# A fused S5 block and attention layer: a constant moved from the projection's weights to the inverted softmax divisors, two rows made in two periods, and the opening's last period moved by one

## The chip, the cores and the metric

The kernel runs on one core of a Trainium2 chip. The core has five engines with an instruction queue each: TensorE for matrix products (PE in the profile; PEld are its weight loads), VectorE (DVE), ScalarE (ACT), GpSimd (POOL) and SyncE (SP), which here issues all DMA transfers. The metric is device time in microseconds (us) of one execution. The kernel before takes 3392.98 us, the median of 3 runs that span 3391.85 to 3394.76 us.

## The reference

Input x is (2, 2048, 512), two sequences of 2048 rows, with a condition vector of 512 for each. The first layer is a state-space block with a feed-forward part. The second layer, whose last stages the change touches, is attention with a layer norm whose scale and shift depend on the condition:

```python
h = _sln(hidden, w, ...)                      # layer norm, * gamma(w) + beta(w)
q, k, v = split of h @ Wqkv.T + bqkv          # 16 heads of 32
energy = einsum('bhqd,bhkd->bhqk', q, k)
att = softmax(energy, axis=-1) / D ** 0.5     # D = 512: after the softmax
out = einsum('bhqk,bhkd->bhqd', att, v)
out = out @ Wp.T + bp
h1 = out + hidden
h2 = _sln(h1, w, ...)                         # the same gamma and beta again
return h2 + h1
```

The factor 1/sqrt(D) comes after the softmax. It is a plain constant on the result of attention, and can be multiplied in anywhere between the softmax and the sum with `hidden`.

## The kernel before

**The opening half.** The S5 block, its feed-forward part and the projections to q, k and v go over 8 chunks of 512 rows, 4 for each sequence. It ends a little after 1340 us. What is left then of the projections (4 value tiles of the chunk before the last, then for the last chunk 4 transposed feature tiles, 8 tiles of keys and queries and 4 value tiles: 20 pieces in the list `left`) is done in the first periods of the attention, beside it.

**Attention.** A block is one sequence, one pair of heads and one chunk of 512 queries; there are 2 * 8 * 4 = 64 blocks. Each block needs 16 tiles of scores (128 keys by two heads by 512 queries). Since fp32 scores need a maximum before the exponential, the scores are made ahead:

- `keep` (line 863) makes a score tile on TensorE (`raw_scores`, line 853), copies it to memory on ScalarE (line 867) and takes the running maximum on VectorE (line 872). Eleven of 16 tiles are kept so.
- `compare` (line 874) does the maximum only, for the other five (line 876). These five are made a second time later, in `make` (line 906), which takes the maximum off while VectorE reads the scores (line 910).
- `turn_run` (line 878) transposes the running maximum on TensorE (line 884) and reduces it on VectorE (line 885), for each head of the pair. `spread` (line 889) transposes the 8 rows of maxima (`pt_neg`, line 892), copies them on ScalarE (line 894), writes them to DRAM (`flat`, line 896) and reads them back to all partitions (`shift`, line 898).
- `take_off` (line 902) adds `shift` to a kept tile on GpSimd (line 904), `exponentials` (line 913) is ScalarE's exp (line 915), and `weighted` (line 918) is the product with the values on TensorE (line 925), with a column of ones, so that the softmax divisor comes out of the same product. The last product of a block is copied out (line 934), and its sums and rows go to DRAM (lines 938, 941).

**Periods.** The order of the work on all engines is written out by hand: a loop over periods j (line 1311), 8 periods to a block (`NP = 8`), with the scores made 14 periods ahead of the products (`AHEAD = 14`). Each engine takes its instructions in this order. Within a period: what `after` put there (`run_due(j)`, line 1329), `make`, `compare`, the first exponential, the kept tiles, then pieces of `left`, the second exponential, what `closing` put there (`run_due(j + 0.5)`, line 1356), `take_off` for the next period and `weighted` for the last one. The loop starts at j = -22; block n has its products from j = 8n on. At `j == OPEN`, with `OPEN = -4`, the memory of the first half is given back (line 1314), new pools are opened, and two value tiles get their ones (line 1323). The pieces of `left` are spread evenly over the periods up to `OPEN` (line 1346). For block 0, `turn_run` is due in j = -5 and -4, and `spread` in j = -3.

**The end of each sequence.** When all heads of a chunk of queries are done, `fetch_sums` (line 953) reads the 16 x 512 divisors back as a 128 x 64 tile; `invert` (line 961), two periods later, takes their reciprocal on VectorE (line 963) and writes it to DRAM (line 964). `fetch`, `divide` and `project` (lines 975 to 1006) read attention's rows and the inverse divisors, multiply them on GpSimd, and project with `wp` on TensorE. `last_rows` (line 946) makes two tiles of 128 equal rows from the layer norm's scale and shift: `along_rows` (line 166) is 4 matmuls that spread columns along rows (line 170) into a PSUM tile and one ScalarE copy (line 174). In this stage that PSUM tile has the tag `pt`, of one buffer, which `turn_run`, `spread` and `project` use too. `last_rows` comes in period 272 for the first sequence (ahead of the period's scores) and in period 483 for the second, where a `turn_run` and an `invert` are due as well. The last chunk of all has its own `end_*` functions: its last pair of heads is divided straight from PSUM in `end_last` (line 1151; lines 1162 and 1164).

**The weights.** `wp`, the 512 x 512 projection laid out as 128 x 2048, is loaded in period 22 (line 1326), and in period 32 GpSimd multiplies all of it by 1/sqrt(D) (line 1328).

Of the kernel before, what the change touches and what calls it, by code (L numbers as in the profile page):

```python
# [8 lines left out]
F32 = mybir.dt.float32  # L9
# [5 lines left out]
ALU = mybir.AluOpType  # L15
# [4 lines left out]
P = 128  # L20
# [19 lines left out]
def tile_s5_block_then_sln_attention(  # L40
# [21 lines left out]
    nc = tc.nc  # L62
    NB, L, D = x.shape
    KC = D // P
# [7 lines left out]
    NQ = L // CH  # L72
# [25 lines left out]
    s_scale = const.tile([P, KC, NB], F32, name="s_scale")  # L98
    s_shift = const.tile([P, KC, NB], F32, name="s_shift")
# [66 lines left out]
    def along_rows(dst, cols, psum, tag):  # L166

        pt = psum.tile([P, CH], F32, name="pt_ar", tag=tag)
        for k in range(KC):
            nc.tensor.matmul(  # L170
                pt[:, k * P : (k + 1) * P], cols[k].to_broadcast([P, P]), ident,
                start=True, stop=True,
            )
        nc.scalar.copy(dst, pt)
# [501 lines left out]
    pt = ps1.tile([P, KC, CH], F32, name="pt_s", tag="po", bufs=1)  # L676
# [266 lines left out]

    held, ending = {}, {}

    def last_rows(b):
        g_row = rows.tile([P, D], F32, name="g_row", bufs=1)
        along_rows(g_row, [s_scale[:, k, b : b + 1] for k in range(KC)], ps, "pt")
        t_row = rows.tile([P, D], F32, name="t_row", bufs=1)
        along_rows(t_row, [s_shift[:, k, b : b + 1] for k in range(KC)], ps, "pt")  # L950
        ending[b] = g_row, t_row

    def fetch_sums(b, c, heads=slice(0, NH), width=64):

# [6 lines left out]
    def invert(b, c, heads=slice(0, NH), width=64):  # L961
        sm = held.pop((b, c, "sm"))
        nc.vector.reciprocal(sm, sm)
        nc.sync.dma_start(invd[b][heads, c * CH : (c + 1) * CH].rearrange("h (s i) -> h s i", i=width), sm)

    def store(b, qt, rows):
# [184 lines left out]
    def end_last(o):  # L1151
        raw, inv = (spare(n)[:, 0, :] for n in ("raw4", "inv4"))
        on = ends["o"][1][:, 1, :]
        turned = ps.tile([P, 2, 2 * P], F32, name="turned", tag="pt")
        parts = [slice(2 * i * P, 2 * (i + 1) * P) for i in range(2)]
        for at in parts:
            nc.scalar.copy(raw[:, at], o[:, at])
        end_begin(1)
        for i, at in enumerate(parts):
            nc.tensor.matmul(turned[:, i, :], ends["turn"], raw[:, at], start=True, stop=True)  # L1160
        for i, at in enumerate(parts):
            nc.vector.reciprocal(inv[:, at], turned[:, i, :])
            for r in (slice(0, HD), slice(3 * HD, P)):
                nc.vector.tensor_tensor(on[r, at], o[r, at], inv[r, at], ALU.mult)
        end_project(1, list(range(NG - 1)))
        mv = small.tile([P, TT, 2], F32, name="mv4")
        g_row, t_row = ending[LB]
        for i in range(2):
            for t in (2 * i, 2 * i + 1):
                nc.tensor.matmul(  # L1170
                    ends["py", i][:, t % 2, :], on[:, t * P : (t + 1) * P], ends["w"], start=False, stop=True
                )
            for t in (2 * i, 2 * i + 1):
                st = small.tile([P, 6], F32, name="st3")
                nc.vector.bn_stats(st, ends["py", i][:, t % 2, :])
                nc.vector.bn_aggr(mv[:, t, :], st)
        v = small.tile([P, TT], F32, name="v4")
        scale = small.tile([P, TT], F32, name="scale4")
        nc.vector.tensor_scalar(v, mv[:, :, 1], EPS, None, ALU.add)
        nc.vector.tensor_scalar(  # L1180
            scale.bitcast(I32), v.bitcast(I32), -0.5, float(0x5F3759DF), ALU.mult, ALU.add
        )

        nc.gpsimd.tensor_scalar(v, v, -0.5, None, ALU.mult)
        for _ in range(3):
            c = small.tile([P, TT], F32, name="c4")
            nc.gpsimd.tensor_tensor(c, scale, scale, ALU.mult)
            nc.gpsimd.tensor_tensor(c, c, v, ALU.mult)
            nc.gpsimd.tensor_scalar(c, c, 1.5, None, ALU.add)
            nc.gpsimd.tensor_tensor(scale, scale, c, ALU.mult)  # L1190
        ws, hts = [spare("w01"), spare("w23")], [spare("ht01"), spare("ht23")]
        for t in range(TT):
            h = ends["py", t // 2][:, t % 2, :]
            w, ht = ws[t // 2][:, t % 2, :], hts[t // 2][:, t % 2, :]
            nc.vector.scalar_tensor_tensor(w, h, mv[:, t, 0:1], g_row, ALU.subtract, ALU.mult)
            nc.vector.tensor_tensor(ht, h, t_row, ALU.add)
        for t in range(TT):
            qt = LC * TT + t
            w, ht = ws[t // 2][:, t % 2, :], hts[t // 2][:, t % 2, :]
            nc.vector.scalar_tensor_tensor(ht, w, scale[:, t : t + 1], ht, ALU.mult, ALU.add)  # L1200
            nc.sync.dma_start(out[LB, qt * P : (qt + 1) * P, :], ht)
# [6 lines left out]
    NP = 8  # L1208
# [20 lines left out]
    def after(j, what, *args):  # L1229

        due.setdefault(j, []).append((what, args))

    def closing(j, what, *args):

        due.setdefault(j + 0.5, []).append((what, args))

    N = len(blocks)
    FIRST = -AHEAD - 8
    OPEN = -4
    for i, n in enumerate(opens):  # L1240
        free = NP * (max(m for m in range(N) if pair_of[m] == i - 2) + 1) if i > 1 else FIRST
        after(max(free if i > 1 else FIRST, NP * n - 26), load_k, i)
        after(max(OPEN + 2, NP * n - 9), load_v, i)
    for n in range(N):
        after(max(FIRST + 1 + n, NP * n - 21), load_q, n)
        after(NP * n - AHEAD + NP + 1, turn_run, n, 0)
# [2 lines left out]
    for b in range(NB):  # L1249
        for c in range(NQ):  # L1250
            j = NP * (blocks.index((b, NPAIR - 1, c)) + 1) + 1
            if (b, c) == (LB, LC):
                most, rest = slice(0, NH - 4), slice(NH - 4, NH - 2)
                j = NP * (N - 1)
                after(j - 5, fetch_sums, b, c, most)
                after(j - 3, invert, b, c, most)
                for g in range(NG - 1):
                    after(j - 2 + g, end_sums, g)
                after(j + 1, end_weights)
                after(j + 1, end_sums_more)  # L1260
                after(j + 2, end_x)
                after(j + 1, fetch_sums, b, c, rest, 32)
                after(j + 4, invert, b, c, rest, 32)
                after(j + 5, end_divisors, NG - 1, 2, 1)
                for g in range(NG - 1):
                    after(j + 3 + g, end_divide, g)
                for e in (1, 2):
                    after(j + 8, end_divide, NG - 1, slice(HD * e, HD * e + HD))
                after(j + 6, end_begin, 0)
                for g in range(NG - 1):  # L1270
                    after(j + 6 + g // 2, end_project, 0, [g])
                continue
            after(j, fetch_sums, b, c)
            after(j + 2, invert, b, c)
            if c == 0:
                after(j + 2, last_rows, b) if b == LB else after(NP * (NPAIR * NQ * (b + 1) + 2), last_rows, b)
            for t in range(TT):
                qt = c * TT + t
                if b == LB:
                    k = j + 3 + 2 * t  # L1280
                    after(k, fetch, b, qt)
                    after(k + 2, divide, b, qt)
                    after(k + 3, project, b, qt)
                    after(k + 3, residual, b, qt)
                    after(k + 3, statistics, b, qt)
                    after(k + 4, deviation, b, qt)
                    after(k + 5, last_norm, b, qt)
                    after(k + 6, last_close, b, qt)
                else:

                    k = NP * (NPAIR * NQ * (b + 1) + 2 + 3 * qt // 2)
                    after(k, fetch, b, qt)
                    after(k + 3, divide, b, qt)
                    for g in range(NG):
                        closing(k + 5 + g // 2, project, b, qt, (g,))
                    closing(k + 7, residual, b, qt)
                    closing(k + 8, statistics, b, qt)
                    closing(k + 9, gain, b, qt)
                    after(k + 11, turns, b, qt)
                    closing(k + 12, scaled, b, qt)  # L1300
                    after(k + 14, close, b, qt)
# [9 lines left out]
    for j in range(FIRST, NP * N + 2):  # L1311
# [12 lines left out]
            wp = fixed.tile([P, KC, D], F32, name="wp")  # L1324
        if j == 2 * NP + 6:
            nc.sync.dma_start(wp, w_pT.rearrange("(k p) f -> p k f", p=P))
        if j == 4 * NP:
            nc.gpsimd.tensor_scalar(wp, wp, ISQ, None, ALU.mult)
        run_due(j)
        n, i = block_at(j + AHEAD)  # L1330
        todo = list(keeps[i]) if n is not None else []
# [90 lines left out]
```

## Time and profile before

| | |
|---|---|
| median of 3 runs | 3392.98 us (3391.85 to 3394.76) |
| the profiled execution | 3393.83 us, of which its span is 3392.1 us |
| mean granted clock of TensorE | 0.992 |
| busy share of the span | PE 97%, DVE 65%, POOL 62%, ACT 58% |
| attention: first product with the values | at 1422.9 us of the span |
| GpSimd's `take_off`, line 904 | 704 instructions, mean 2390 ns |
| scores, line 856 / products, line 925 | 2688 matmuls, mean 427 ns / 4096 matmuls, mean 611 and 597 ns |
| multiplication of `wp`, line 1328 | 1 instruction, 5369 ns, at 1531.7 us |
| rows of `last_rows`, ScalarE's copies | at 2382.9 and 2384.7, 3201.4 and 3203.3 us |
| reciprocals of `invert`, line 963 | 9 instructions, median 543 ns |
| division in `end_last`, line 1164 | 4 instructions, 412 to 430 ns, from 3372.4 us |

How to read the profile: a page has the busy time of each engine over the span, slices, the chain that ended last, and groups of instructions with a mean duration and the idle time before them. A timeline lists instructions in order of time. Its columns are the start and the time in us, the engine, the line of the kernel, the operation, what is written and read, the shapes and the count; a bracket at the end gives how long the engine sat idle before it, and what it waited for. Matmuls in a timeline are pipelined, so a group's time reaches somewhat into the next one's.

### The profile page before, as it was taken

Reading aid. Unit: us, or ns where it says so; the run is one execution under the profiler, and the core shown is the slowest. Engines: PE = TensorE matmul, PEld = TensorE weight load, DVE = VectorE, ACT = ScalarE, POOL = GpSimd, SP = SyncE. Lnnn points to the kernel's source line nnn. Section 1 sums busy time; section 2 is a strip of 40 time slices with the busy share of each in tenths; the row PEclk is TensorE's granted clock in tenths of the full one; section 3 lists DMA queues with packets and bytes.
Section 4 is the critical chain, followed back from the end, with each engine's and each line's share of the span. In section 5 each row is a group of like instructions: output and inputs, shape, how many; then the busy total and the mean of one; then the engine's idle time right before and its main releaser. Section 6 shows DMA issues by size and latency. Waiting matters only on the chain.

```text
span 3392.1 us, 33637 instructions
## 1 busy us (share of the span) xinstructions
PE 3294.7 (97%) x11076; PEld 1417.8 (42%) x11076; DVE 2218.2 (65%) x2792; ACT 1951.0 (58%) x2210; POOL 2117.6 (62%) x1164
## 2 busy tenths in 40 slices
PE   7999999999999999999999999999999999999987
PEld 4444444444444444443444444444444434443432
DVE  5352525252525212688888888888888888888884
ACT  2111111111111111598999999999888888888852
POOL 2341313131313111399999999999899999989885
PEclk9999999999999999999999999999999999999998
DMA  8022221222222212332313231323233243243233
GB/s 298 25 50 71 53 75 49 78 57 71 62 62 56 59 47 75 113 85 61 74 49 74 67 74 49 75 68 75 70 92 90 67 95 88 65 90 83 63 102 97
DMA packets 249781, 259.07 MB, mean 76 GB/s; under 512 B 94920, under 2 KB 167112, under 8 KB 245510
## 3 DMA queue, kind: packets, MB, share of 16 engines
q1 hardware_dynamic: 249606, 256.92, 28.5%
q8 instruction: 88, 1.44, 0.2%
q14 instruction: 87, 0.71, 0.1%
HBM read 166.77 MB, written 67.76 MB: 69 GB/s over the span
## 4 chain that ended last, share of the span: by engine, by line
PE 62%; DVE 15%; ACT 15%; issue 3%; POOL 2%; DMA 2%; SPq 0%; DVEq 0%; ACTq 0%; POOLq 0%
PE ph L538 13%; PE po L551 13%; PE o L925 10%; DVE run L872 8%; PE s L856 8%; ACT x L867 7%; PE pk L587 6%; ACT x L915 4%; ACT pT L915 4%; PE pv L599 3%; DVE pT L910 3%; PE py L1005 2%; POOL x L904 2%; DVE run L876 2%; PE pu L474 2%
## 5 line engine op out<-in xcount | busy, mean ns | idle before, releaser
L904 POOL TENSOR_TENSOR x<-x,shift 128x1024 f32<-128x1024 f32 x704 | 1654.9, 2390 | 134.1 <-DMA shift<-flat 117.1
L856 PE MATMUL s<-qs,ks 128*128 128x512 f32 x2688 | 824.8, 427 | 39.4 <-DVE run L872 26.6
L867 ACT COPY x<-s 128x1024 f32<-128x1024 f32 x704 | 692.2, 1011 | 142.9 <-PE s L856 137.1
L872 DVE TENSOR_TENSOR run<-s,run 128x1024 f32<-128x1024 f32 x576 | 705.2, 1224 | 81.7 <-ACT x L867 37.1
L915 ACT ACTIVATE x<-x 128x1024 f32<-128x1024 f32 x704 | 738.8, 1059 | 15.7 <-POOL x L904 15.4
L925 PE MATMUL o<-x,v 128*64 128x512 f32 x2816 | 717.2, 611 | 1.2 <-ACT x L915 1.2
L856 PEld LDWEIGHTS s<-qs,ks 128*128 128x128 f32 x2688 | 444.1, 189 | 454.7 <-DVE run L872 158.0
L538 PE MATMUL ph<-fT,w_sb 128*128 128x512 f32 x1024 | 459.4, 592 | 0.9 <-ACT fT L682 0.9
L551 PE MATMUL po<-w_sb,hid 128*128 128x512 f32 x1024 | 460.0, 592 | 0.0
L542 ACT ACTIVATE hid<-ph,vec 128x512 f32<-128x512 f32 x128 | 87.8, 686 | 614.7 <-PE ph L538 614.7
L910 DVE TENSOR_TENSOR pT<-s,shift 128x1024 f32<-128x1024 f32 x320 | 388.9, 1215 | 52.6 <-PE s L856 52.2
L876 DVE TENSOR_TENSOR run<-s,run 128x1024 f32<-128x1024 f32 x320 | 389.3, 1216 | 12.1 <-PE s L856 11.6
L915 ACT ACTIVATE pT<-pT 128x1024 f32<-128x1024 f32 x320 | 339.5, 1061 | 89.9 <-DVE pT L910 89.6
L561 POOL TENSOR_TENSOR x<-x,gated 128x512 f32<-128x512 f32 x32 | 39.6, 1269 | 506.5 <-DVE gated L560 506.5
L925 PE MATMUL o<-pT,v 128*64 128x512 f32 x1280 | 332.0, 597 | 15.2 <-ACT pT L915 15.2
L164 DVE SCALAR_TENSOR_TENSOR lo<-pk,vec,hi 128x512 fp32r<-128x512 f32 x64 | 47.8, 746 | 423.0 <-ACT hi L163 423.0
L551 PEld LDWEIGHTS po<-w_sb,hid 128*128 128x128 f32 x1024 | 194.4, 190 | 243.9 <-issue 243.7
L538 PEld LDWEIGHTS ph<-fT,w_sb 128*128 128x128 f32 x1024 | 194.1, 190 | 243.3 <-issue 239.2
L925 PEld LDWEIGHTS o<-x,v 128*64 128x64 f32 x2816 | 157.0, 135 | 311.7 <-issue 239.3
L163 ACT ACTIVATE hi<-pk,vec 128x512 fp32r<-128x512 f32 x64 | 44.0, 687 | 373.4 <-PE pk L587 373.4
L524 POOL TENSOR_TENSOR x<-x,gated 128x512 f32<-128x512 f32 x28 | 35.4, 1264 | 255.3 <-DVE gated L523 255.3
L925 PEld LDWEIGHTS o<-pT,v 128*64 128x64 f32 x1280 | 91.6, 138 | 200.2 <-issue 142.2
(280 smaller groups left out, 2449.3 us busy)
## 6 DMA issues: line engine op xcount, KB each, us to landing
ks<-kd SPq DMA_DIRECT2D x128, 256.0 KB
qs<-qd SPq DMA_DIRECT2D x512, 64.0 KB
shift<-flat SPq DMA_DIRECT2D x64, 512.0 KB
moved<-fT SPq DMA_DIRECT2D x224, 64.0 KB
x<-in_x SPq DMA_DIRECT2D x8, 1024.0 KB
w_sb<-in_w SPq DMA_DIRECT2D x8, 1024.0 KB
kd<-hi SPq DMA_DIRECT2D x32, 256.0 KB
kd<-lo SPq DMA_DIRECT2D x32, 256.0 KB
```

The costliest lines, as they stand in the source:

```text
L538: nc.tensor.matmul(ph, w1_sb[:, k, f * P : (f + 1) * P], fts[b, c][:, k, :], start=k == 0, stop=k == KC - 1)
L551: nc.tensor.matmul(pos[b, c][:, t, :], hid[:, t * P : (t + 1) * P], w2_sb[:, f, :], start=f == 0, stop=f == FC - 1,)
L587: nc.tensor.matmul(pk, w[:, k, g * P : (g + 1) * P], hT[:, k, :], start=k == 0, stop=k == KC - 1)
L599: nc.tensor.matmul(pv, fts[b, c][:, k, t * P : (t + 1) * P], wv[:, k, :], start=k == 0, stop=k == KC - 1)
L856: nc.tensor.matmul(s[:, e, :], kst[pair_of[n], e][:, kt * P : (kt + 1) * P], qst[n][:, e, :], start=True, stop=True,)
L867: nc.scalar.copy(x, s)
L872: nc.vector.tensor_tensor(runs[n], s, kept[n, 0] if kt == 1 else runs[n], ALU.max)
L876: nc.vector.tensor_tensor(runs[n], raw_scores(n, kt), runs[n], ALU.max)
L904: nc.gpsimd.tensor_tensor(x, x, shifts[n], ALU.add)
L910: nc.vector.tensor_tensor(x, s, shifts[n], ALU.add)
L915: nc.scalar.activation(x, x, AF.Exp)
L925: nc.tensor.matmul(outs[n][64 * e : 64 * e + 64, :], v[:, kt, e : e + 2, :], x[:, e, :], start=first, stop=final,)
```

## The change

Four edits. The multiplication of `wp` by `ISQ` = 1/sqrt(D) is gone; `invert` multiplies the reciprocals by `ISQ`, and `end_last` multiplies by it in its own division. `last_rows` becomes `last_row`, called once for each row: the first in the closing part of period k, the second in the closing part of period k + 1, where k is 272 for the first sequence, as before, and 481 for the second, two periods ahead of before. `OPEN` goes from -4 to -3, so that the pieces of `left` have one period more, and the pools of the attention are opened one period later; the first loads of values stay in period -2 (`OPEN + 1` in place of `OPEN + 2`).

```diff
-    def last_rows(b):
-        g_row = rows.tile([P, D], F32, name="g_row", bufs=1)
-        along_rows(g_row, [s_scale[:, k, b : b + 1] for k in range(KC)], ps, "pt")
-        t_row = rows.tile([P, D], F32, name="t_row", bufs=1)
-        along_rows(t_row, [s_shift[:, k, b : b + 1] for k in range(KC)], ps, "pt")
-        ending[b] = g_row, t_row
+    def last_row(b, name, columns):
+        row = rows.tile([P, D], F32, name=name, bufs=1)
+        along_rows(row, [columns[:, k, b : b + 1] for k in range(KC)], ps, "pt")
+        ending.setdefault(b, []).append(row)
...
         nc.vector.reciprocal(sm, sm)
+        nc.vector.tensor_scalar(sm, sm, ISQ, None, ALU.mult)
         nc.sync.dma_start(invd[b][heads, c * CH : (c + 1) * CH].rearrange("h (s i) -> h s i", i=width), sm)
...
             for r in (slice(0, HD), slice(3 * HD, P)):
-                nc.vector.tensor_tensor(on[r, at], o[r, at], inv[r, at], ALU.mult)
+                nc.vector.scalar_tensor_tensor(
+                    on[r, at], o[r, at], ISQ, inv[r, at], ALU.mult, ALU.mult
+                )
...
-    OPEN = -4
+    OPEN = -3
...
-        after(max(OPEN + 2, NP * n - 9), load_v, i)
+        after(max(OPEN + 1, NP * n - 9), load_v, i)
...
             if c == 0:
-                after(j + 2, last_rows, b) if b == LB else after(NP * (NPAIR * NQ * (b + 1) + 2), last_rows, b)
+
+                k = j if b == LB else NP * (NPAIR * NQ * (b + 1) + 2)
+                closing(k, last_row, b, "g_row", s_scale)
+                closing(k + 1, last_row, b, "t_row", s_shift)
...
-        if j == 4 * NP:
-            nc.gpsimd.tensor_scalar(wp, wp, ISQ, None, ALU.mult)
```

## What is predicted

> **What bounds the kernel now.** I read the page first. TensorE is busy nearly all the time, and no other engine passes two thirds:
>
> ```profile
> PE 3294.7 (97%) x11076; PEld 1417.8 (42%) x11076; DVE 2218.2 (65%) x2792; ACT 1951.0 (58%) x2210; POOL 2117.6 (62%) x1164
> ```
>
> A change to another engine is therefore worth what it does to TensorE's gaps and nothing else. To find them I took from TensorE's timeline the one transpose that each block of attention has, `pt_neg`. Its distance from block to block is a ruler: 28.11 to 28.16 us where nothing happens, so I use 28.12 as the undisturbed block.
>
> ```profile
> 1521.13 0.27 PE L892 MATMUL pt_neg<-ident,neg 128*8 128x128 f32 x1
> 1553.24 0.27 PE L892 MATMUL pt_neg<-ident,neg 128*8 128x128 f32 x1
> 1582.43 0.27 PE L892 MATMUL pt_neg<-ident,neg 128*8 128x128 f32 x1
> 1610.57 0.27 PE L892 MATMUL pt_neg<-ident,neg 128*8 128x128 f32 x1
> ```
>
> These blocks last 32.11, 29.19 and 28.14 us. The first has the multiplication of `wp`. The same ruler gives 31.36 us for the block with the two rows of sequence 0 (2372.07 to 2403.43), 32.02 for that of sequence 1 (3178.22 to 3210.24), and 28.51, 28.68, 28.53 and 28.51 for the four blocks in which sequence 0's divisors are inverted. These are the places that the change touches, besides the opening and the last 20 us.
>
> **Part 1: the pass over `wp` goes.** The timelines of GpSimd, ScalarE and TensorE:
>
> ```profile
> 1531.68 5.37 POOL L1328 TENSOR_SCALAR wp<-wp 128x2048 f32<-128x2048 f32 x1
> 1537.13 21.08 POOL L904 TENSOR_TENSOR x<-x,shift 128x1024 f32<-128x1024 f32 x9
> ```
>
> ```profile
> 1539.53 1.06 ACT L915 ACTIVATE x<-x 128x1024 f32<-128x1024 f32 x1 [4.16 <-POOL x L904]
> ```
>
> ```profile
> 1540.64 1.08 PE L925 MATMUL o<-x,v 128*64 128x512 f32 x4 [1.24 <-ACT x L915]
> 1542.50 1.08 PE L925 MATMUL o<-pT,v 128*64 128x512 f32 x4 [0.78 <-ACT pT L915]
> 1546.52 0.73 PE L856 MATMUL s<-qs,ks 128*128 128x512 f32 x2 [1.42 <-DVE run L872]
> ```
>
> `take_off` stands behind the 5.37 us, the exponential behind `take_off`, the products and VectorE's maxima behind ScalarE. The block is 32.11 - 28.12 = 3.99 us too long. Behind it nothing is late: a block on, GpSimd waits 3.41 us for a transfer again, as in ordinary blocks. So the whole 3.99 us come back. Here a rule speaks against the gain: the Trainium skill ("GPSIMD Engine Reference", section 3.1) puts a GpSimd body with at most 2 operations at 1.03 cycles per element, so 2048 elements at the page's 1.2 GHz are an estimated 1.76 us. ScalarE would then have waited 4.16 - 3.61 = 0.55 us, TensorE about nothing, and the edit were worth 0. The row says 5.37 us, and it decides. The next block's extra 1.07 us is another thing: there the small write of the maxima took 3.16 us from issue to the next issue, and 1.2 to 1.35 in nearly all other blocks. I take it for chance and leave it out: the profiled execution is 3393.83 us (span 3392.1 and 1.7 around it), 0.85 above the median.
>
> **Part 2: the two rows in two periods.** Before, both stand together and share one PSUM buffer:
>
> ```profile
> 2383.55 1.16 PE L170 MATMUL pt_ar<-ident,s_shift 128*128 128x128 f32 x8 [0.68 <-ACT g_row L174]
> 2389.83 0.73 PE L856 MATMUL s<-qs,ks 128*128 128x512 f32 x2 [0.60 <-DVE run L872]
> 3200.23 1.16 PE L170 MATMUL pt_ar<-ident,s_scale 128*128 128x128 f32 x8 [1.29 <-DVE neg L885]
> 3202.07 1.16 PE L170 MATMUL pt_ar<-ident,s_shift 128*128 128x128 f32 x8 [0.68 <-ACT g_row L174]
> ```
>
> The work itself, 2 * 0.91 = 1.82 us (2383.55 to the next start, 2384.46, for one), stays. The rest of the excess is waiting: 31.36 - 28.12 - 1.82 = 1.42 us for sequence 0, and 32.02 - 28.12 - 1.82 = 2.08 for sequence 1. After: the rows stand behind the scores of their periods, so VectorE and ScalarE have work while TensorE makes them. For sequence 0 (periods 272 and 273) no other user of the buffer comes before 275: the 1.42 go. For sequence 1 (481 and 482) the second row's copy is queued on ScalarE behind the second exponential of 482, and the next `pt_run`, in 483, waits for it. In an ordinary block that exponential ends some 0.9 us after the place of `pt_run`; with the row's own 0.91 of TensorE time ahead, the copy's 0.59 is left as a wait of about 0.6. Gain 2.08 - 0.6 = 1.5. Sum: 2.9 us; between 0 (each wait comes back elsewhere) and 3.5.
>
> **Part 3: the multiplication after the reciprocal.** Nine small VectorE instructions are new, none of that shape is in the trace. From below: `tensor_scalar` on 128x1 takes 0.153 us (line 1027). From above: the reciprocal on the same tile, 0.54. `tensor_scalar` on 128x512 takes 0.546 (line 147), so on a line 64 elements are 0.20, nearer the low end; dependent ones start 0.04 after the end of the one before, and the reciprocal's overlap with its successor (0.08) is lost: 0.24 each. Who pays for it is seen at the reciprocals themselves:
>
> ```profile
> 2251.58 0.54 DVE L963 RECIPROCAL sm<-sm 128x64 f32<-128x64 f32 x1
> 2252.04 1.16 DVE L910 TENSOR_TENSOR pT<-s,shift 128x1024 f32<-128x1024 f32 x1
> ```
>
> ```profile
> 2255.71 0.72 PE L856 MATMUL s<-qs,ks 128*128 128x512 f32 x2 [0.47 <-DVE run L872]
> ```
>
> VectorE loses 0.46 us, and the four blocks are 0.39 to 0.56 longer: it passes to TensorE one to one, through `pT` and the maxima that are queued behind it. So 4 * 0.24 for sequence 0. Of sequence 1's five, the first lies right behind the new rows, which give VectorE 1.8 us of room: 0. The second, third and fourth stand ahead of a `pT` for which TensorE waits: 3 * 0.24. The fifth (32x32, at 3344.9) has nobody behind it for 3 us. Sum 1.7 us; from 0 to 2.2 (all nine). The write of the inverse on SP's queue goes 0.24 later too; behind it stands only `out` or the next `flat`, 1 us or more away, but in one block (3303.97), which is counted.
>
> **Part 4: the last division.**
>
> ```profile
> L1164 DVE TENSOR_TENSOR o<-o,inv x4: 412/420/430, 3372.4 to 3375.5; 32x256 f32<-32x256 f32 x4
> ```
>
> Four of these become `scalar_tensor_tensor`. On 128x512 that form takes 0.742 us (line 1047) where `tensor_tensor` takes 0.681 (line 1048), both out of PSUM: 0.06 more, 0 to 0.06 on half the length. All four lie on the chain that ends the kernel: +0.2, from 0 to 0.25.
>
> **Part 5: the opening.**
>
> ```profile
> 1407.33 0.27 PE L892 MATMUL pt_neg<-ident,neg 128*8 128x128 f32 x1
> 1422.92 2.78 PE L925 MATMUL o<-x,v 128*64 128x512 f32 x8
> ```
>
> Between these TensorE has only scores, and waits for the first `shift`: ScalarE's copy of the maxima at 1408.88 (behind two copies of scores), `flat` issued at 1409.16, `shift` at 1410.42, GpSimd from 1414.76. By the order of instructions the change moves one key/query piece behind the next scores and each of the four value pieces a period on; the last now stands right ahead of `pt_neg`. TensorE's work before `pt_neg` is the same to the matmul, so the hole is not filled. I laid the pieces out with their durations (value piece 3.43, `pt_run` 0.44, scores 0.43 to 0.46 a matmul): the last value piece ends at 1406.85, its eviction (0.69, same PSUM buffer) at 1407.54, `pt_neg` at 1407.6. That is 0.3 later, but ScalarE's two copies are then done, and `flat` goes at 1408.15, 1.0 earlier. Against that, on SP's queue the last value tile's write (256 KB) now goes 0.6 ahead of `flat` in place of 3.7, so that `flat` may land behind it. I take a gain of 0.3, and -2 to +5.7 (below) as ends. The memsets follow 2 us later; the first value loads keep their place behind `shift`, and the DMA engines are idle from 1420 on, some 3 us ahead of the first product: no cost.
>
> The clock is the other thing here: the granted clock falls to 0.50 from 1412 to 1424:
>
> ```profile
> 1412.00:1416.00 4.00, 3.66 (x6) 1.50 (x6) 3.67 (x3) 3.08 (x3) 1.24 (x1) 0.50 0.97 206
> ```
>
> The Trainium skill ("TensorE: Matmul & The Clock Gate", Part 1) says that an idle window of about 3.4 us halves the clock, and a busy one as long restores it. If the hole were filled, the scores and products of 1420.4 to 1424.3 would gain about 2 us. But the hole stays, so I count 0.
>
> **Sum.** -3.99 - 2.9 + 1.7 + 0.2 - 0.3 = -5.3 us, 0.16%. Against the profiled execution 3388.5, without its chance 1.07 us 3387.5; against the median 3392.98 - 5.3 = 3387.7, say 3387.6.
>
> **The rivals.**
> - A, as above: 3386.4 to 3389.0. Chance 0.60.
> - B, more than that: the inversions' multiplications hide (1.7), and the opening's 1.0 comes whole (0.7 more): 3385.2; with a restored clock 3383. For: VectorE is 65% busy. Against: the four long blocks. Chance 0.18.
> - C, a wait in place of the one removed: copies of the rows stand behind exponentials, and `pt_run` or the scores wait as long as before: 3387.6 + 2.9 = 3390.5. For: `pt` has one buffer. Against: two periods of distance in sequence 0. Chance 0.14.
> - D, slower than before: `flat` lands behind the last value tile's write. In the last block, where `flat` is behind other transfers, it takes 4.76 us instead of 1.26: 3.5 later, GpSimd too, and the scores and products at half clock for one window more, 2.2. With the lost 0.3: 3387.6 + 6.0 = 3393.6. It decides from a distance `flat` to `shift` of about 4 us on. Against: 256 KB are not so much. Chance 0.08.
>
> A measurement of this kernel can tell about 0.2% (6.8 us) from no change: faster means below 3386.2. B lies there nearly whole, and a tenth of A's cases: 0.25. Slower by as much, over 3399.8, needs D and more: 0.04. Between: 0.71. For 8 in 10 the range takes A, most of B and most of C: 3384.2 to 3390.6.
>
> **What would show it.** Right: the `wp` block at 28.1 to 28.5 us on the ruler; the blocks of the rows at 30.0 and 30.6, without a wait of `pt_ar`; the four blocks of inversions at 28.7 to 28.9; the last division at 0.42 to 0.48 each; `flat` near 1408.2 and the first product near 1422.6. Wrong: a `flat` to `shift` distance over 2 us in the opening, `pt_run` waiting over 1 us for a row's copy, or new waits in the last three blocks, where VectorE waits for the output's transfers and I assumed that all of it only moves.

## The result, and the profile after

| | before | after |
|---|---|---|
| median (range; runs) | 3393.54 us (3390.67 to 3396.28; 14) | 3397.88 us (3392.82 to 3417.72; 14) |
| ratio of after to before | | 1.0021, 95% interval 1.0011 to 1.0031 |
| the profiled execution (span) | 3393.83 us (3392.1) | 3404.93 us (3403.1) |
| mean granted clock | 0.992 | 0.991 |

The change makes the kernel slower, by 4.3 us between the medians and by 7 us between the means (the ratio weighs the high runs too), where 5.3 us less were forecast. The profiled execution of after lies 7.05 us above its median, so what is read in it is too large by about that much. The spread is a result too: 24.9 us from lowest to highest, 5.6 before. The page of after:

```profile
PE 3294.0 (97%) x11076; PEld 1418.8 (42%) x11076; DVE 2234.0 (66%) x2801; ACT 1951.4 (57%) x2210; POOL 2113.0 (62%) x1163
```

TensorE and GpSimd have, but for the one removed instruction, the same work. VectorE has 9 instructions more and 15.8 us more to do. At the forecast's 0.20 us each, the nine multiplications would have been 1.8. The ruler again, `pt_neg` on TensorE's timeline (block k of the ruler lasts from the k-th `pt_neg` to the next):

```profile
1522.36 0.27 PE L892 MATMUL pt_neg<-ident,neg 128*8 128x128 f32 x1
1550.50 0.27 PE L892 MATMUL pt_neg<-ident,neg 128*8 128x128 f32 x1
...
2285.61 0.27 PE L892 MATMUL pt_neg<-ident,neg 128*8 128x128 f32 x1
2324.56 0.27 PE L892 MATMUL pt_neg<-ident,neg 128*8 128x128 f32 x1
```

The block that had the pass over `wp` now lasts 28.13 us. But one of the four blocks with an inversion lasts 38.95. All places at which the two rulers differ by over 0.2 us:

| place | before | after | difference |
|---|---|---|---|
| start to the first `pt_neg` | 1407.33 | 1409.67 | +2.34 |
| block 1 (the opening) | 29.08 | 27.97 | -1.11 |
| block 5 (`wp`) | 32.11 | 28.13 | -3.98 |
| block 6 / block 18 (a slow write of the maxima) | 29.19 / 28.39 | 28.27 / 29.06 | -0.92 / +0.67 |
| blocks 30 to 33 (inversions, sequence 0) | 28.51, 28.68, 28.52, 28.52 | 29.29, 29.66, 38.95, 30.60 | +14.27 |
| block 35 (rows, sequence 0) | 31.36 | 29.11 | -2.25 |
| block 61 (rows and an inversion, sequence 1) | 32.02 | 30.64 | -1.38 |
| blocks 62 and 63 (inversions) | 41.79, 43.22 | 42.40, 43.62 | +1.01 |
| last `pt_neg` to the end | 96.80 | 99.53 | +2.73 |

They add up to 11.4 us, where the spans differ by 11.1; differences under 0.2 us make up the rest. Of the first row 1.6 us are there before 120 us of the span, in the loading, where the change touches nothing.

Block 32, on VectorE's timeline of after, then GpSimd's, then TensorE's:

```profile
2308.05 9.07 DVE L962 TENSOR_SCALAR sm<-sm 128x64 f32<-128x64 f32 x1
2317.04 1.21 DVE L910 TENSOR_TENSOR pT<-s,shift 128x1024 f32<-128x1024 f32 x1
```

```profile
2291.37 25.70 POOL L904 TENSOR_TENSOR x<-x,shift 128x1024 f32<-128x1024 f32 x11 [2.63 <-DMA shift<-flat]
```

```profile
2318.30 3.68 PE L856 MATMUL s<-qs,ks 128*128 128x512 f32 x6 [8.11 <-DVE pT L910]
```

The multiplication of 64 columns takes 9.07 us, and it ends at 2317.12; GpSimd's eleventh and last `take_off` of the block ended 0.05 us earlier, at 2317.07. Everything behind it on VectorE stands still, `pT` first, and TensorE waits 8.11 us for `pT`. Then it pays a second time, because its clock fell in the wait: 0.50 is granted from 2313.3 to 2323.5. These are windows of all engines; the last numbers of a line are the granted clock, the DMA share and GB/s:

```profile
2309.00:2313.00 4.00, 1.19 (x8) 0.42 (x4) 4.00 (x1) 0.00 (x0) 4.00 (x3) 1.00 0.00 0
...
2317.00:2321.00 4.00, 2.59 (x5) 1.25 (x6) 3.90 (x5) 2.26 (x3) 0.07 (x1) 0.50 0.04 8
```

So a stall of 9.07 us makes the block 38.95 - 28.52 = 10.43 us longer.

The other parts, on TensorE's timeline of after: the two rows of sequence 1, and the first product with the values.

```profile
3202.05 1.05 PE L170 MATMUL pt_ar<-ident,s_scale 128*128 128x128 f32 x8
...
3205.94 1.05 PE L170 MATMUL pt_ar<-ident,s_shift 128*128 128x128 f32 x8
...
3209.14 0.66 PE L884 MATMUL pt_run<-ident,run 128*128 128x128 f32 x4 [0.28 <-ACT t_row L174]
```

```profile
1409.67 0.27 PE L892 MATMUL pt_neg<-ident,neg 128*8 128x128 f32 x1 [0.79 <-DVE vt L607]
...
1424.26 2.69 PE L925 MATMUL o<-x,v 128*64 128x512 f32 x8
```

The rows stand apart and wait for nothing; of the wait of about 0.6 us that I foresaw for the next `pt_run`, 0.28 are there. `pt_neg` of the opening waits 0.79 us for the last value tile's eviction, as foreseen.

### The profile page after: what moved, and what is told of

The parts are those of the page before. It is cut to its first block, busy times and chain, and to the rows that moved or that the text cites. A ratio compares the mean times of both kernels' runs of the same rounds, so it can differ in the third digit from the quotient of the medians.

```text
span 3403.1 us, 33642 instructions
## 1 busy us (share of the span) xinstructions
PE 3294.0 (97%) x11076; PEld 1418.8 (42%) x11076; DVE 2234.0 (66%) x2801; ACT 1951.4 (57%) x2210; POOL 2113.0 (62%) x1163
## 4 chain that ended last, share of the span: by engine, by line
PE 62%; DVE 16%; ACT 16%; issue 3%; DMA 2%; POOL 1%; SPq 0%; DVEq 0%; ACTq 0%; POOLq 0%
PE ph L538 13%; PE po L551 13%; PE o L925 10%; DVE run L872 8%; PE s L856 8%; ACT x L867 7%; PE pk L587 6%; ACT x L915 4%; ACT pT L915 4%; PE pv L599 3%; DVE pT L910 3%; PE py L1004 2%; DVE run L876 2%; PE pu L474 2%; PE pt_run L884 1%
```

## The theory and the experiments

**Theory 1.** The multiplication reads and writes SBUF, the memory that GpSimd works in as well, and it cannot begin while a GpSimd instruction holds a way into that memory which the two engines share. All nine in after start while GpSimd is busy, and all nine end 31 to 53 ns behind the end of a GpSimd instruction. **Rivals:** the removed pass over `wp`, the new place of the rows or the new opening makes the later blocks longer; or any small instruction added there costs that much.

The Trainium skill ("SBUF — State Buffer", section "Who interferes with whom") has the rule behind the theory: VectorE and GpSimd share one pair of ports under an exclusive lock; `tensor_scalar` from SBUF to SBUF can use it (in a two-port mode), an instruction with two SBUF inputs too (against a GpSimd instruction that reads SBUF, as `take_off` does), and whoever issues first holds the pair for the whole instruction while the other blocks. The nine ends agree with this. By the rule a wait lasts at most one GpSimd instruction, here 2.39 us. The 9.07 does not agree: the multiplication missed three GpSimd ends and was let in at the fourth.

| kernel | median (range; runs) | before beside it | ratio, 95% interval |
|---|---|---|---|
| 1: no multiplication | 3385.67 (3381.76 to 3388.66; 10) | 3394.02 | 0.9975, 0.9966 to 0.9984 |
| 2: only a multiplication | 3407.34 (3403.61 to 3415.70; 4) | 3394.02 | 1.0046, 1.0031 to 1.0061 |
| 3: on ScalarE | 3386.45 (3382.71 to 3388.14; 10) | 3394.02 | 0.9977, 0.9968 to 0.9986 |
| 4: six forms | 3452.85 (1) | 3394.02 | |
| 5: as 1, opening as before | 3384.81 (3382.20 to 3387.74; 10) | 3392.42 | 0.9977, 0.9968 to 0.9987 |
| 6: as 1, rows as before | 3389.88 (3387.83 to 3393.41; 13) | 3392.42 | 0.9993, 0.9984 to 1.0001 |
| 7: multiplication in GpSimd's idle time | 3392.36 (3387.16 to 3397.91; 12) | 3392.42 | 1.0000, 0.9992 to 1.0009 |
| 8: only the constant moved | 3389.76 (3388.30 to 3391.07; 13) | 3392.42 | 0.9989, 0.9981 to 0.9998 |
| 9: GpSimd's instruction halved | 3688.42 (1) | 3393.83 | |
| 10: input from PSUM | 3413.35 (1) | 3395.22 | |

**1. The constant in the value tiles' column of ones.** After, but with no multiplication at all: the column that gives the softmax divisor holds sqrt(D), so the inverted divisors carry 1/sqrt(D) by themselves.

```diff
-                nc.gpsimd.memset(v[:, :, 1, :], 1.0)
+                nc.gpsimd.memset(v[:, :, 1, :], float(D) ** 0.5)
...
-        nc.vector.tensor_scalar(sm, sm, ISQ, None, ALU.mult)
...
-                nc.vector.scalar_tensor_tensor(
-                    on[r, at], o[r, at], ISQ, inv[r, at], ALU.mult, ALU.mult
-                )
+                nc.vector.tensor_tensor(on[r, at], o[r, at], inv[r, at], ALU.mult)
```

> The changed kernel, but the factor comes in through the column of ones in the value tiles: it is set to sqrt(D), so that the divisors come out of the product sqrt(D) times larger and the reciprocals need no multiplication. VectorE's nine new multiplications are gone and the last division is as before; the rows and the opening stay changed. Theory 1 (the nine multiplications wait for GpSimd's instruction in progress, or for a later one): the four blocks in which sequence 0's divisors are inverted go from 29.3, 29.7, 39.0 and 30.6 us to the 28.5 to 28.7 of before, and the kernel, with 4.0 (pass over wp), 3.6 (rows) and 0.4 (opening) saved, takes 3385.5, about 0.24% less than before, with runs spread over no more than before's 6 us. Rival (the rows or the opening made it slower): stays within 3 us of the 3397.9 of the changed kernel, or scatters as widely.

Measured: less than before, and 12.2 us less than after by the medians. Blocks 30 to 33 are at 28.51, 28.64, 28.51 and 28.52 us, as before. The rest of the change does no harm; the multiplications do all of it.

**2. Only a multiplication.** Before, with a multiplication by 1.0 behind each reciprocal.

```diff
         nc.vector.reciprocal(sm, sm)
+        nc.vector.tensor_scalar(sm, sm, 1.0, None, ALU.mult)
```

> The kernel before, with one edit: after each of the nine reciprocals VectorE multiplies the same tile by 1.0. Theory 1: the added instruction alone makes the slowdown and the scatter: 0.2 to 9 us for one, 3398 to 3415 in all, other runs far apart, and each one's end falls within 0.1 us of the end of a GpSimd instruction. Rival (rows or opening): 1.7 us more than before, as was forecast for the instruction alone, 3395.3, at 0.2 us for each.

Measured: 13.3 us more than before by the medians, for nine instructions. Their durations (ns, least/median/largest) in after, and then in this kernel:

```profile
L962 DVE TENSOR_SCALAR sm<-sm x9: 181/674/9070, 2249.1 to 3356.1; 128x64 f32<-128x64 f32 x7, 96x64 f32<-96x64 f32 x1, 32x32 f32<-32x32 f32 x1
```

```profile
L964 DVE TENSOR_SCALAR sm<-sm x9: 291/1896/2379, 2251.9 to 3357.0; 128x64 f32<-128x64 f32 x7, 96x64 f32<-96x64 f32 x1, 32x32 f32<-32x32 f32 x1
```

The cost is there without any other part of the change. Here too each ends 33 to 56 ns behind a GpSimd end.

**3. The multiplication on ScalarE.** After, with one line changed.

```diff
-        nc.vector.tensor_scalar(sm, sm, ISQ, None, ALU.mult)
+        nc.scalar.mul(sm, sm, ISQ)
```

> The changed kernel with the nine multiplications on ScalarE in place of VectorE. Theory 1: no wait for GpSimd; about 0.25 us for each, and some cost where it stands ahead of exponentials: 3385 to 3388 us, runs close together. Rival (the dependence on the reciprocal that it follows in place, or the path through DRAM behind it, costs the time): the four blocks stay above 29 us, since the chain reciprocal, multiplication, transfer is no shorter.

Measured: 11.4 us less than after by the medians, level with 1. The nine take 228 to 257 ns on ScalarE:

```profile
L962 ACT ACTIVATE sm<-sm x9: 228/257/257, 2250.2 to 3339.3; 128x64 f32<-128x64 f32 x7, 96x64 f32<-96x64 f32 x1, 32x32 f32<-32x32 f32 x1
```

What costs is not that a small instruction stands between the reciprocal and the write, but which engine runs it.

**4. Six forms of instruction.** Before, with one VectorE instruction on private tiles at the start of the fourth period of blocks 1 to 59 (the loop's numbers, from 0; the ruler's are one higher); the form goes round with the block's number. Nobody reads the tiles.

```diff
+        if n % 6 == 0:
+            nc.vector.tensor_scalar(a, a, 1.0, None, ALU.mult)
+        elif n % 6 == 1:
+            nc.vector.tensor_scalar(a[:, :1], a[:, :1], 1.0, None, ALU.mult)
+        elif n % 6 == 2:
+            nc.vector.tensor_tensor(a, a, probe[1], ALU.max)
+        elif n % 6 == 3:
+            nc.vector.reciprocal(a, a)
+        elif n % 6 == 4:
+            nc.vector.tensor_scalar(a[:, :8], a[:, :8], 1.0, None, ALU.mult)
+        else:
+            nc.vector.scalar_tensor_tensor(a, a, 1.0, probe[1], ALU.mult, ALU.mult)
```

> The kernel before, with one small VectorE instruction more in each of 59 blocks, at the start of period 8n+3 while GpSimd works through its queue; six forms in turn, on a private tile of 128x64: tensor_scalar 128x64, tensor_scalar 128x1, tensor_tensor of two tiles in memory 128x64, reciprocal 128x64, tensor_scalar 128x8, scalar_tensor_tensor of two tiles in memory 128x64. Theory 1 with the skill's rule (contention in a two-port mode or with two inputs in memory): both tensor_scalar over 1 element and the two-input forms wait, 0.2 to 9 us with ends at GpSimd's; 128x1 and the reciprocal don't: 0.15 and 0.54. Rival (dependence on the instruction just ahead): none of the forms waits, since none follows its producer: 0.15 to 0.3 for all but the reciprocal.

Measured, in the groups of this kernel:

```profile
L1246 DVE TENSOR_SCALAR probe<-probe x10: 142/144/146, 1458.0 to 3101.6; 128x1 f32<-128x1 f32 x10
L1248 DVE TENSOR_TENSOR probe<-probe,probe x10: 618/1046/1603, 1486.2 to 3134.0; 128x64 f32<-128x64 f32 x10
L1250 DVE RECIPROCAL probe<-probe x10: 541/543/544, 1515.1 to 3167.7; 128x64 f32<-128x64 f32 x10
L1252 DVE TENSOR_SCALAR probe<-probe x10: 162/692/1711, 1547.6 to 3196.3; 128x8 f32<-128x8 f32 x10
L1254 DVE SCALAR_TENSOR_TENSOR probe<-probe,probe x10: 224/1262/10895, 1575.8 to 3226.2; 128x64 f32<-128x64 f32 x10
L1244 DVE TENSOR_SCALAR probe<-probe x9: 205/1777/1962, 1617.1 to 3071.8; 128x64 f32<-128x64 f32 x9
```

The two forms that my bounds came from, `tensor_scalar` on one column and the reciprocal, are the two that do not wait: their least and largest differ by 3 or 4 ns. All the others wait, eight columns as well as 64, and each ends shortly behind a GpSimd end (48 to 54 ns for 64 columns, 79 to 88 with two inputs). So not any added instruction costs this; the form decides. One was let in only at the fifth GpSimd end, after 10.9 us.

**5 and 6. The opening and the rows by themselves.** Kernel 1 with one more part undone: in 5 the opening (the first diff), in 6 the rows (the second), of which both come again in one period ahead of its scores.

```diff
-    OPEN = -3
+    OPEN = -4
...
-        after(max(OPEN + 1, NP * n - 9), load_v, i)
+        after(max(OPEN + 2, NP * n - 9), load_v, i)
```

```diff
-                closing(k, last_row, b, "g_row", s_scale)
-                closing(k + 1, last_row, b, "t_row", s_shift)
+                k = j + 2 if b == LB else k
+                after(k, last_row, b, "g_row", s_scale)
+                after(k, last_row, b, "t_row", s_shift)
```

> The version with the factor in the column of ones, with the opening set back (OPEN = -4, the first value loads at OPEN + 2). My forecast's step: the later opening is worth 0.3 us, so this run is 0 to 1 us slower than that version, 3385.7 to 3386.7, and the first maxima's transpose and the block after it together are about 0.4 us longer, counted from the last matmul of the feed-forward stage. Rival (the opening costs, since the last value tile's write goes ahead of the small write): 2 to 6 us faster.

> The version with the factor in the column of ones, with the two rows set back: both in period 272, and both in period 483, ahead of the scores. Step of the forecast: the split is worth 2.9 us, by the blocks of the changed kernel 2.25 for the first sequence and 1.4 to 1.9 for the second. So 3389.4, with blocks of 31.3 and 32.0 us in place of 29.1 and 30.2. Rival (waits come back elsewhere): no slower than the version it comes from.

Measured: 5 and 1 have nearly the same ratio, so the opening is too small to see in the times. 6 lies 5.1 us above 5, measured together; the ruler says 31.36 and 32.03 us for the rows' blocks, against 29.12 and 30.16 in kernel 1, 4.1 us in sum. The rows are worth that. The other 1.0 us stays open: 6 has the new opening and 5 has not, so a gain from the opening would make it larger, not explain it.

**7. The multiplication in GpSimd's idle time.** After, with the inversions of sequence 0 three periods later, where GpSimd waits for the next block's `shift`.

```diff
-            after(j + 2, invert, b, c)
+            after(j + (2 if b == LB else 5), invert, b, c)
```

> The changed kernel, with the inversions of sequence 0 (reciprocal, multiplication and write) three periods later, where GpSimd stands idle for 3.4 us and waits for the next block's shift. Theory 1 (VectorE waits for GpSimd's instruction in progress): these four multiplications take about 0.1 to 0.2 us each, the four blocks 28.3 to 28.8 us, the kernel about 3388 to 3392, since the four of sequence 1 still wait. Rival (something in the multiplication itself): as slow as the changed kernel.

Measured: the four take 194 to 196 ns, what I had put for them, and their blocks (now 31 to 34) 28.70 to 28.72 us. The first of them on VectorE's timeline:

```profile
2255.33 0.54 DVE L961 RECIPROCAL sm<-sm 128x64 f32<-128x64 f32 x1
2255.91 0.20 DVE L962 TENSOR_SCALAR sm<-sm 128x64 f32<-128x64 f32 x1
2256.02 1.22 DVE L910 TENSOR_TENSOR pT<-s,shift 128x1024 f32<-128x1024 f32 x1
```

From the reciprocal's start to `pT` it is 0.69 us, 0.23 more than before. The five of sequence 1 stay where they were and take 276 to 2389 ns. That leaves the time at 1.0000 of before: by the ratios 7.1 us less than after, 8.5 more than 1.

**8. Only the constant moved.** Before, with the column of sqrt(D) of kernel 1 and without the pass over `wp`; rows and opening as before.

```diff
-                nc.gpsimd.memset(v[:, :, 1, :], 1.0)
+                nc.gpsimd.memset(v[:, :, 1, :], float(D) ** 0.5)
...
-        if j == 4 * NP:
-            nc.gpsimd.tensor_scalar(wp, wp, ISQ, None, ALU.mult)
```

> The kernel before, with the factor in the column of ones and the pass over wp gone; rows and opening as before. Step of the forecast: 3.99 us, in the one block that goes from 32.11 to 28.1. So 3389.7 beside 3393.7. If GpSimd's pass was partly hidden: less than 3; if the next block's 1.07 us belonged to it too: 5.1, with a next block of 28.2 in each run.

Measured: block 5 is at 28.11 us, 4.0 less. By the medians it is 2.7 us, by the ratio 3.7 with an interval of 0.7 to 6.4 that holds the 4.0. Block 6 is at 29.26 us here, as in before, so its slow write is no effect of the pass.

**9. GpSimd's instruction halved.** Before, with one multiplication of a private 128x64 tile at the start of the fourth period of blocks 1 to 59, and with `take_off` in two halves in odd blocks.

```diff
-            nc.gpsimd.tensor_tensor(x, x, shifts[n], ALU.add)
+            if n % 2:
+                for e in range(2):
+                    nc.gpsimd.tensor_tensor(x[:, e, :], x[:, e, :], shifts[n][:, e, :], ALU.add)
+            else:
+                nc.gpsimd.tensor_tensor(x, x, shifts[n], ALU.add)
...
+            after(NP * n + 3, times_one)
```

> The kernel before, with one VectorE tensor_scalar (times 1.0) on a private 128x64 tile at the start of the fourth period of blocks 1 to 59, and with take_off of the odd blocks in two GpSimd instructions of 128x512 in place of one of 128x1024. Nobody reads the private tile. Theory 1 (the instruction waits for the end of the GpSimd instruction in progress): each instruction that starts while GpSimd is busy ends about 0.05 us after a GpSimd end, and the waits go with the length of GpSimd's instruction: even blocks mean about 1.2 us and mostly up to 2.4, odd blocks mean about 0.6 us and mostly up to 1.3; where an end is missed, the wait is longer by whole GpSimd instructions. Rival (a stall with a price of its own, whatever GpSimd's instruction is): the same distribution in even and odd blocks, and no fixed distance to GpSimd's ends in the odd ones. By Theory 1 the time of the run is about 58 times 0.5 to 1 us above the kernel before, some 3420 to 3450 us, since nearly all of them stand ahead of a tile for which TensorE waits.

Measured: 3688.42 us, far above both. Two of the 59 on VectorE's timeline, in the loop's blocks 19 (odd) and 20 (even), and GpSimd's timeline beside them:

```profile
2054.53 12.12 DVE L1245 TENSOR_SCALAR probe<-probe 128x64 f32<-128x64 f32 x1
...
2096.25 1.02 DVE L1245 TENSOR_SCALAR probe<-probe 128x64 f32<-128x64 f32 x1
```

```profile
2051.81 14.79 POOL L906 TENSOR_TENSOR x<-x,shift 128x512 f32<-128x512 f32 x12
...
2080.74 21.15 POOL L908 TENSOR_TENSOR x<-x,shift 128x1024 f32<-128x1024 f32 x9 [14.14 <-DMA shift<-flat]
```

The second was let in at the first GpSimd end, in the middle of nine `take_off`. The first was let in when GpSimd's twelve were done. The 59 fall into these two kinds with nothing between them:

| | let in at the first end (one at the second) | only when GpSimd had nothing more queued |
|---|---|---|
| even blocks (GpSimd's instruction 2.39 us) | 25: mean 1.05, largest 2.16 us | 4: mean 10.2 us, at the 4th to 6th end |
| odd blocks (1.29 us) | 15: mean 0.83, largest 1.40 us | 15: mean 12.6 us, at the 10th to 12th end |

In all 19 of the long kind GpSimd's next instruction starts 12.6 to 15.2 us later. So Theory 1 holds for where the waits end (48 to 58 ns behind a GpSimd end in 57 of 59), and for the short kind, whose largest value follows GpSimd's instruction. It had the long kind wrong: halving the instruction made the sum worse, not better, because the long waits came in 15 of 30 in place of 4 of 29. The rival's fixed price falls as well. The 19 long ones last 230 us together; the kernel is 295 us longer than before, and of that the halved `take_off` may have a part, too.

**10. The input from PSUM.** Before, with the same multiplication behind the third `pT` of each block; the input is the private tile in even blocks, the scores' PSUM tile in odd ones.

```diff
         nc.vector.tensor_tensor(x, s, shifts[n], ALU.add)
+        if kt == NX + 2 and 0 < n < N - 4:
+            nc.vector.tensor_scalar(probe, s[:, 0, :64] if n % 2 else probe, 1.0, None, ALU.mult)
```

> The kernel before, with one VectorE tensor_scalar of 128x64 (times 1.0, onto a private tile that nobody reads) behind the third pT of blocks 1 to 59. In even blocks it reads the private tile (SBUF to SBUF, as the change's multiplication does), in odd blocks the first 64 columns of the scores in PSUM that the pT before it read. GpSimd's work is untouched. Theory 1 in its narrow form (only an instruction that takes all its operands from SBUF, and writes to SBUF, needs the memory port that GpSimd holds): odd blocks 0.14 to 0.2 us each, with no fixed distance to GpSimd's ends; even blocks as the even ones of the run before (each end some 0.05 us behind the end of a GpSimd instruction, mean 1 us where the first end lets it in, 8 to 12 us in one of seven). Rival (any added instruction of this size stalls VectorE beside a busy GpSimd): the same waits in both.

Measured, in the groups of this kernel:

```profile
L912 DVE TENSOR_SCALAR probe<-s x30: 212/215/217, 1465.5 to 3200.9; 128x64 f32<-128x64 f32 x30
L912 DVE TENSOR_SCALAR probe<-probe x29: 184/679/2452, 1493.7 to 3171.6; 128x64 f32<-128x64 f32 x29
```

From PSUM, 30 of 30 take 0.21 us, 26 of them begun while GpSimd was busy. From SBUF they wait. Whether the instruction writes in place does not decide it: line 147, shown below, writes another tile than it reads, and it waits. The long kind does not occur here, where GpSimd mostly was in its block's last `take_off`: there is no further instruction to lose to. By the Trainium skill ("VectorE: DVE Perf Modes", section "Why PSUM operands drop a tier") a PSUM operand rules the two-port mode out; the 0.21 us agree. Together with the rule on two SBUF inputs above it also fits that before had no trouble in attention: `run` and `pT`, VectorE's main work there, read scores from PSUM and only one operand from SBUF, and all 1280 of them in before take 1.16 to 1.23 us.

## Why the prediction was wrong, step by step

**Part 1, `wp`: right.** Forecast -3.99, the block -3.98 (kernel 8: -4.00). Leaving the next block's 1.07 out was right too, since kernel 8 has it without the pass; that it is chance is not shown (in kernel 8 it is the same block, and in after and kernels 1, 3 and 6 it is block 18). The row, not the page's rule, decided it.

**Part 2, the rows: right in its mechanism, too small.** Forecast 1.42 + 1.5; in kernel 1, free of the multiplications, 31.36 - 29.12 = 2.24 and 32.02 - 30.16 = 1.86. For sequence 0 the term that was off is the work itself, of which the prediction said that it "stays", 1.82 us. I took the rows' own time for a full addition to the block. Behind scores, part of it falls into time that TensorE would have lost anyway: the block is only 29.11 - 28.12 = 0.99 us longer than an empty one. By the starts in kernel 1's trace, the rows take 1.97 us there, and the block's 42 score matmuls 11.36 us, where the empty block before it has 12.31. For sequence 1 the block is 2.04 us longer than an empty one, so the work stays whole; there the term that was off is the wait left at `pt_run`, 0.6 by forecast and 0.28 in after.

**Part 3, the multiplications: wrong, and it decides the sign.** Forecast +1.7, "from 0 to 2.2 (all nine)"; the runs say +12.2 (after against 1) and +13.3 (2 against before) by the medians, 15.6 in both by the ratios (1.0021 - 0.9975 = 0.0046, and 1.0046). Who pays was read rightly: it passes to TensorE through `pT`, whole, and in a long wait with a clock of 0.50 on top. The failed step is the cost of one multiplication: "none of that shape is in the trace", and then "0.20, nearer the low end" between 0.153 and 0.54. It left the wait for GpSimd at nothing, without a reason. Kernel 7 shows that the 0.24 was right where GpSimd is idle (0.23; the overlap of 0.08 that the forecast calls lost, but does not count, is there behind the multiplication); beside a busy GpSimd the nine cost 12.2 / 9 = 1.4 us each on average. Both ends of the bound came from instructions that do not wait for GpSimd, as kernel 4 shows; and the third row, "`tensor_scalar` on 128x512 takes 0.546 (line 147)", was a median. This is the whole row in the groups of before, and beside it line 118, a form with four columns:

```profile
L147 DVE TENSOR_SCALAR xn<-x,mean,rstd x96: 539/546/1503, 22.3 to 1346.7; 128x512 f32<-128x512 f32 x96
...
L118 DVE TENSOR_SCALAR rstd<-ln_v x24: 170/170/1194, 20.3 to 1342.3; 128x4 int32<-128x4 int32 x24
```

The largest is 2.8 and 7 times the median: 28 of the 96 took 1.48 to 1.50 us, and six of the 24 took 1.19. One of those six on VectorE's timeline of before, and GpSimd's beside it:

```profile
221.40 1.19 DVE L118 TENSOR_SCALAR rstd<-ln_v 128x4 int32<-128x4 int32 x1
```

```profile
221.30 1.26 POOL L512 TENSOR_TENSOR x<-x,r_shift 128x512 f32<-128x512 f32 x1
```

It starts 0.10 us into a GpSimd instruction and ends 0.03 behind it. All 34 began while GpSimd was busy, and none of the short ones did. So the trace of before did show the wait, in the opening half. What it cost TensorE there was not measured, and I read medians for an attention in which GpSimd is busy 25.7 of 28 us. An estimate from this row: a wait of half a `take_off`, 1.2 us, eight times, some +10 us in place of 1.7, and about +3 in the sum in place of -5.3. The long kind is not to be had from that trace: those 28 + 6 were all let in at the first end. One of the two that the forecast put at 0 was not free either: behind the new rows the multiplication takes 0.385 us, and block 61 is 30.64 us, against 30.16 in kernel 1.

**Part 4, the last division: too careful.** Forecast +0.2; the group in after:

```profile
L1163 DVE SCALAR_TENSOR_TENSOR o<-o,inv x4: 413/421/429, 3383.5 to 3386.6; 32x256 f32<-32x256 f32 x4
```

It was 412/420/430. The form costs nothing there.

**Part 5, the opening: about right.** Forecast -0.3. From the start of the feed-forward part's last matmul to the first product the kernels with the new opening take 88.15 to 88.48 us, those with the old 88.34 to 88.68: 0.2, with as much uncertainty. Inside it `flat` went only 0.5 us earlier in after, where 1.0 was forecast (counted from that matmul), and `flat` to `shift` took 1.56 us in place of 1.26 (the sign of rival D was 4). The hole stayed, and D did not come. The times cannot tell.

**The end of the kernel.** I had named new waits in the last three blocks as what would make the forecast wrong. They are there, and again they are multiplications: the eighth takes 2.38 us, at 3312.3, and TensorE waits 5.62 us for the next `pT`, where before and kernel 6 have 3.20 and 3.23. On TensorE's timeline of after, then of before:

```profile
3316.95 1.97 PE L925 MATMUL o<-pT,v 128*64 128x512 f32 x4 [5.62 <-ACT pT L915]
```

```profile
3306.16 1.97 PE L925 MATMUL o<-pT,v 128*64 128x512 f32 x4 [3.20 <-ACT pT L915]
```

This is 2.4 of the tail's 2.73 us. The tail varies from 95.8 to 98.6 us in kernels without multiplications, too; what moves it is not settled.

**The sum.** By the terms as measured: -4.0 - 4.1 - 0.2 = -8.3 without the multiplications (kernel 1: 3394.02 - 3385.67 = -8.4), and with 12.2 to 15.6 for them +3.9 to +7.3 (measured +4.3 by the medians, +7.1 by the ratio). Of the cases A to D none had this in it: the only one on the slower side, D, was about a transfer.

**Still open.** What decides, at a GpSimd end, whether VectorE is let in or loses until GpSimd has nothing queued: 19 of 59 lost in kernel 9, one of nine in after, one of 39 of the waiting forms in kernel 4, none of nine in kernel 2. That a port shared by the two engines is what is waited for is the skill's account, which the forms and the PSUM input agree with; the runs show the wait and where it ends. How far VectorE's instruction stood in GpSimd's does not decide it (0.06 to 1.09 us were left in those that lost, 0.09 to 1.24 in those that won, odd blocks). And that the wide spread of after comes from such draws falling anew in each execution is an inference from the spread of 1 and 3 (6.9 and 5.4 us) against that of 2 and 7 (12.1 and 10.8); only one execution of after has a trace.

## What to carry to other kernels

Before a small instruction is put on VectorE beside a busy GpSimd, see where its operands lie: two inputs in SBUF, or a `tensor_scalar` of more than one column from SBUF to SBUF, can wait for GpSimd, and with it all that is queued behind on VectorE. Read a form's least, median and largest duration, not the median alone; where they lie far apart, look at what the other engines do at that time, and take the bound from a stage in which they do the same as at the new place. And a constant that can be written into data that is set anyway (here a column of ones, kernels 1 and 5: 0.23 to 0.25% under before) needs no instruction at all.

## What was not expected of the hardware

- A VectorE instruction that waits for GpSimd may lose to it again and again: until the 12th GpSimd end, 14.1 us, for a multiplication that takes 0.19 us with GpSimd idle. Shorter GpSimd instructions did not help (15 long waits of 30 with 1.29 us, 4 of 29 with 2.39).
- A small size is no protection: 128x8 waits as 128x64 does (medians 0.69 and 1.78 us), 128x1 does not (0.144), nor does a reciprocal of 128x64 (0.543).
- The same multiplication out of PSUM costs 0.215 us, with GpSimd busy (26 of 30) or idle.
